# Turning half of a softmax's probabilities on VectorE and by copies inside SBUF, in a decoder layer's cross-attention

## The chip, the core and the metric

The kernel runs on one core of one Trainium2 chip. The metric is the device time of one execution in microseconds (us). Engines are named as the profile names them: PE is TensorE (matrix products and transposes), PEld its weight loads, DVE is VectorE, ACT is ScalarE, POOL is GpSimd, SP is SyncE, which here only issues transfers (DMAs). SBUF is the memory on the chip with 128 partitions, PSUM the memory into which PE writes.

## What is computed

One decoder layer in fp32 on `x` of shape (8, 256, 1024), B = 8 batch elements of S = 256 rows, E = 1024 columns, in three stages. Each adds its result to `x` after a layer norm.

```python
x = x + self_attention(layernorm(x))            # 32 heads, weights by their signs
x = x + cross_attention(layernorm(x), ctx)      # 16 heads, low rank
x = x + ffn(layernorm(x))                       # gate and up, 2752 wide, low rank

# cross_attention(Q, K), for one batch element
C_q, C_kv = Q @ Wq_d, K @ Wkv_d                 # 256 x 128, 256 x 64
CqWqk = (C_q @ W_qk).reshape(n, 16, 64)
scores = einsum('nhl,kl->hnk', CqWqk, C_kv) / sqrt(64)
attn = softmax(scores, axis=-1)                 # 16 heads of 256 x 256
V_up = (C_kv @ Wv_u).reshape(nkv, 16, 64)
out = einsum('hnk,khd->nhd', attn, V_up)
```

The kernel multiplies the probabilities by `C_kv` first and by `Wv_u` after that. The matrix product sums over partitions, so the probabilities, which the softmax leaves with the queries n on the partitions, must first be turned so that the keys k lie there. The change is about how they are turned.

## The kernel before

All rows are handled in tiles of P = 128, TB = 2 of them for each batch element. The order of every engine's work is written out by hand: the program records the instructions under a manual schedule, and each engine runs its own in that order, waiting on semaphores where it needs another's result. A transfer counts on one of eight semaphores of its queue kind, used in turn; it waits until the transfer eight places earlier has landed.

**The loop.** The attention of both kinds goes by `step` (L733), one for four heads: 64 steps of self-attention (b = 0 to 7, c = 0 to 7), then 32 of cross-attention (b = 0 to 7, c = 0 to 3), called from the loop at L1658. A step computes the scores of its own four heads (`cur`), turns the probabilities of the step before (`prev`) and finishes the step before that (`due`). In the order of the code, a step of the cross-attention is:

- PE: the scores of four heads, 16 matmuls into four banks `pss0` to `pss3` that have one buffer each (L676); they wait until the exponentials of the step before have read these banks.
- DVE: `due.early()`, a copy of `po` from PSUM to `ol` (L709); then the row maxima `nm` of the four heads (L743).
- PE: `turned` for the four heads of `prev` (L575): four transposes of 128 x 128 each (L579) into `ps_pt`; ACT copies each to SBUF as `pT` (L583), four buffers.
- PE: `due.late()`: `ol` times Wv_u into `ps_o` (L716); DVE multiplies by one over the sums (`y`, L724), POOL adds to the rows `x1t` (L731). `y` has two buffers.
- ACT: eight exponentials with their sums (L762), `cur.p`, mixed with the parts by a count of PE's time (`sc` and `pe`).
- The parts of the plan, from a queue that `cross_plan` (L1501) fills: for the next batch element the turn of the context and of the normed rows by DVE in blocks of 32 x 32 (`turn32`, L185), `ps_k` and `ckv` (L855, L868), `ps_q` and `cq` (L925, L930), `ckvT` (L877, L880), and `ps_qk` and `cqk` (L941, L944), whose copies go to DVE and ACT in turn. c = 0 has two of the four products `ps_qk` and the turn of the context, c = 1 has `ps_k`, c = 2 has `ps_q`, c = 3 has `ckvT` and the other two `ps_qk`. In b = 0, 1 and 2, output projections of the self-attention (L547) come on top, in b = 7 factors of the feed-forward (L1123).
- DVE: one over the sums (L688).
- PE: `prev.weighted` (L693): `po` = turned probabilities times `ckvT`, 16 matmuls (L699).

**Transfers of the cross-attention.** Before the change SP issues all but the stores of finished rows (`x_leave`, L950, on POOL): the context by quarters (`quarters_load`, L168), the rows `x1t` (L831), the copy of each half of `ckv` to the other half's partitions, SBUF to SBUF (L869), the normed rows to DRAM (L894) and back by quarters (L168), and the feed-forward's weights.

**Feed-forward.** It starts after the last step; its `unit`s take the `pT` buffers for `ac2` (L1220).

Of the kernel before, what the change touches and what calls it, by code (L numbers as in the profile page):

```python
# [18 lines left out]
P = 128  # L19
# [16 lines left out]
def decoder_layer(  # L36
# [67 lines left out]
    dve, act = nc.vector.tensor_copy, nc.scalar.copy  # L104

# [59 lines left out]
    def quarters_load(dst, rows, w=EQ):  # L165

        for k in range(Q4):
            nc.sync.dma_start(  # L168
                dst[32 * k : 32 * k + 32],
                rows[:, k * w : (k + 1) * w].rearrange("(a q) e -> q a e", q=32),  # L170
            )

    def rows_load(dst, rows):

        for k in range(Q4):
            nc.sync.dma_start(
# [74 lines left out]
    def load_x(b):  # L251
        out = []
        for t in range(TB):
            xs = xin.tile([P, E], F32, tag="xin", name="xs")
            nc.sync.dma_start(xs, xf[b * TB + t])
# [9 lines left out]
    def scales_load():  # L265
        for gh in range(2):
            nc.sync.dma_start(
# [3 lines left out]
        nc.sync.dma_start(prow[8:10, :], ks.rearrange("(c p) -> c p", p=P))  # L271
        nc.sync.dma_start(prow[10:12, :], vs.rearrange("(c p) -> c p", p=P))
        nc.sync.dma_start(prow[12:20, :], os_.rearrange("(c p) -> c p", p=P))
# [46 lines left out]
    def weight_load(i):  # L320
        a = blocks[i]
        a.w = wk_.tile([P, E], F32, tag=where[i], name="w")
        if a.q:
            gh, r = a.t // 4, a.t % 4
            for j in range(4):
                r0 = ((gh * 4 + j) * 4 + r) * HD
                nc.sync.dma_start(a.w[j * HD : (j + 1) * HD, :], a.rows[r0 : r0 + HD, :])
        elif a.o:

            rows = a.rows[a.t * P : (a.t + 1) * P, :]  # L330
            for c in range(EC):
                nc.sync.dma_start(
# [3 lines left out]
        else:  # L336
            nc.sync.dma_start(a.w, a.rows[a.t * P : (a.t + 1) * P, :])
# [237 lines left out]
    def turned(p):  # L575
# [6 lines left out]
        pT = wk_.tile([P, TB, S], F32, tag="pT", name="pT", bufs=4)  # L582
        nc.scalar.copy(pT, ps)  # L583
        return pT

    class Self:


        def __init__(self, st, c):
            self.st, self.c = st, c  # L590
# [72 lines left out]
    class Cross:  # L663


        def __init__(self, st, c):
            self.st, self.c = st, c
# [25 lines left out]
        def weighted(self, pTs):  # L693

            self.po = pso.tile([P, 2, S], F32, tag="pso", name="po")
            for i in range(2):
                for k in range(TB):
                    for j in range(2):
# [3 lines left out]
                            pTs[2 * i + j][:, k, :],  # L702
# [4 lines left out]
        def early(self):  # L707
            self.ol = wk_.tile([P, 2, S], F32, tag=("oh0a", "oh0b")[self.c % 2], name="ol")
            nc.vector.tensor_copy(self.ol, self.po)  # L709
# [23 lines left out]
    def step(cur, prev, parts, extra=None):  # L733
# [4 lines left out]
        due = prev.prev if prev is not None else None  # L738
        if due is not None:
            due.early()  # L740
        pTs = []
        for j in range(4):
            nc.vector.tensor_reduce(nm[:, j, :], s[j], AX.X, ALU.max, negate=True)  # L743
            if prev is not None:
                pTs.append(turned(prev.p[j]))
# [13 lines left out]
        def exp(j, t):  # L759
# [5 lines left out]
            )  # L765

# [30 lines left out]
        if prev is not None:  # L797
            prev.weighted(pTs)
# [7 lines left out]
    def cross_weights():  # L806
# [9 lines left out]
        nc.sync.dma_start(xw.wqk, wqk)  # L816
        for i in range(2):
            rows_load(xw.wkvd[:, :, i, :], wkvd)
        for j in range(2):
            nc.sync.dma_start(  # L820
# [4 lines left out]
    def cross_x(st):  # L825
# [3 lines left out]
        for t in range(TB):  # L829
            xs = wt.tile([P, E], F32, tag=f"qw{2 * (st.b % 3) + t}", name="x1t")  # L830
            nc.sync.dma_start(xs, x1[st.b * TB + t])  # L831
# [17 lines left out]
    def ckv_part(st):  # L849
        def main():  # L850
# [14 lines left out]
            for t in range(TB):  # L865
# [3 lines left out]
                nc.sync.dma_start(st.ckv[there, cols], st.ckv[here, cols])  # L869
# [14 lines left out]
    def lnx_parts(st):  # L884

        def send(t):
            need(st)
            g = st.b * TB + t
            for h in range(2):
# [4 lines left out]
                nc.sync.dma_start(n2[g][:, h * 512 : (h + 1) * 512], xn)  # L894
# [22 lines left out]
    def cq_part(st):  # L917
        box = {}

        def main(half):  # L920
# [7 lines left out]
            if half:  # L928
                st.cq = wk_.tile([P, S], F32, tag="v", name="cq", bufs=2)
                nc.vector.tensor_scalar_mul(st.cq, ps, 1.0 / 8.0)  # L930
# [920 lines left out]
```

## Time and profile before

| | us |
|---|---|
| median of 3 runs | 1462.55 |
| lowest and highest | 1459.47, 1462.96 |
| the profiled execution, its own time | 1462.0 |
| its span, first to last instruction | 1460.2 |

| engine | busy us | share of the span |
|---|---|---|
| PE | 1422.7 | 97% |
| DVE | 1073.5 | 74% |
| PEld | 954.7 | 65% |
| ACT | 849.6 | 58% |
| POOL | 610.5 | 42% |

The page gives each engine's busy time, then groups of equal instructions: line, engine, operation, output<-input, shapes, count, then busy time and mean duration of one, then idle time ahead of them and what ended it. The timeline lists an engine's instructions in order of time: start, duration, engine, line, operation, count, and in brackets the idle time before and what released it. Matmuls overlap one another, so the duration of one is longer than the time from one to the next. The mean granted clock of PE is 0.993 of full speed. The scores of the cross-attention start between 629.1 and 948.7 us, and its last `po` ends at 974.

### The profile page before, as it was taken

How to read it: one execution, taken by the hardware profiler on the slowest of the kernel's cores; microseconds unless marked ns; L12 is line 12 of the kernel's file. 1: busy time of each engine (PE TensorE's matmuls, PEld its weight loads, DVE VectorE, ACT ScalarE, POOL GpSimd, SP SyncE). 2: the span in 40 equal slices, each digit the busy share in tenths (PEclk: the TensorE clock that was granted, in tenths of full speed). 3: DMA queues.
4: the chain of work that ended last, by engine and by line, in shares of the span. 5: the costliest groups of instructions: out<-in, count | busy, mean ns of one | idle time of the engine just before them, and what ended most of it. 6: DMA issues, size and time to landing. Idle time of an engine off the chain costs nothing.

```text
span 1460.2 us, 25787 instructions
## 1 busy us (share of the span) xinstructions
PE 1422.7 (97%) x8946; PEld 954.7 (65%) x8946; DVE 1073.5 (74%) x2042; ACT 849.6 (58%) x2553; POOL 610.5 (42%) x769
## 2 busy tenths in 40 slices
PE   6899999999999999989999999999999999999998
PEld 6778888888888888667787777654444444444444
DVE  6888898989898989866777778447747645555664
ACT  4777898989898988856556666543313322223320
POOL 2544444444444443402232262435525424555740
PEclk9999999999999999989999999999999999999999
DMA  9620010101010124344448676723222000213003
GB/s 213 135 59 16 30 59 30 59 30 59 31 62 27 45 63 163 105 103 130 134 128 271 199 249 175 230 89 131 84 61 72 29 0 34 82 58 129 1 0 116
DMA packets 102961, 134.75 MB, mean 92 GB/s; under 512 B 44538, under 2 KB 75440, under 8 KB 102704
## 3 DMA queue, kind: packets, MB, share of 16 engines
q1 hardware_dynamic: 98224, 116.33, 27.2%
q0 software_dynamic: 4608, 16.78, 3.0%
q8 instruction: 72, 1.18, 0.3%
q14 instruction: 57, 0.47, 0.1%
HBM read 90.60 MB, written 41.94 MB: 91 GB/s over the span
## 4 chain that ended last, share of the span: by engine, by line
PE 54%; ACT 2%; DVE 2%; DMA 1%; issue 1%; SPq 0%; POOL 0%; ACTq 0%; DVEq 0%
PE c L1189 17%; PE z L1283 9%; PE ps_pt L579 4%; PE ps_o L1399 4%; PE s L676 4%; PE ps_p L1123 4%; PE po L699 3%; PE ps_o L716 2%; PE ps_q L925 2%; PE ps_qk L941 2%; ACT p L762 2%; PE ps_k L855 1%; PE ps_o L547 1%; PE ps_h L1252 0%; DMA n<-xn 0%
## 5 line engine op out<-in xcount | busy, mean ns | idle before, releaser
L762 ACT ACTIVATE p<-s,nm 128x256 f32<-128x256 f32 x768 | 358.4, 518 | 3.3 <-DVE nm L743 3.3
L583 ACT COPY pT<-ps_pt 128x512 f32<-128x512 f32 x384 | 197.7, 600 | 146.1 <-PE ps_pt L579 146.1
L743 DVE TENSOR_REDUCE nm<-s 128x2 f32<-128x512 f32 x384 | 237.5, 679 | 5.0 <-PE s L676 3.7
L579 PE MATMUL ps_pt<-ident,p 128*128 128x128 f32 x1536 | 198.9, 282 | 5.8 <-DVE p L623 2.5
L579 PEld LDWEIGHTS ps_pt<-ident,p 128*128 128x128 f32 x1536 | 167.4, 143 | 46.2 <-issue 24.2
L762 ACT ACTIVATION_READ_ACCUMULATOR p<-s,nm 128x1 f32 x768 | 191.8, 250 | 0.0
L1240 POOL TENSOR_TENSOR ac<-ac,sg 128x512 f32<-128x512 f32 x41 | 52.2, 1273 | 207.5 <-ACT sg L1239 207.5
L731 POOL TENSOR_TENSOR x1t<-x1t,y 128x256 f32<-128x256 f32 x64 | 46.3, 743 | 200.5 <-DVE y L724 200.5
L407 POOL TENSOR_SCALAR tmp<-y 128x512 f32<-128x512 f32 x78 | 60.1, 770 | 167.4 <-DVE y L556 91.3
L1189 PE MATMUL c<-t,s_v 128*128 128x512 f32 x252 | 122.2, 594 | 1.1 <-ACT q L1213 0.8
L454 PE MATMUL ps_q<-xh,qT_w 128*128 128x256 f32 x496 | 122.4, 288 | 0.0
L454 PE MATMUL ps_q<-xl,qT_w 128*128 128x256 f32 x496 | 119.6, 282 | 0.0
L1199 ACT COPY a<-c 128x512 f32<-128x512 f32 x42 | 24.6, 585 | 153.6 <-PE c L1189 153.6
L547 PE MATMUL ps_o<-oT_w,oh 128*128 128x512 f32 x256 | 106.4, 416 | 0.0
L547 PE MATMUL ps_o<-oT_w,ol 128*128 128x512 f32 x256 | 101.7, 397 | 0.0
L454 PEld LDWEIGHTS ps_q<-xh,qT_w 128*128 128x128 f32 x496 | 93.5, 188 | 1.6
L454 PEld LDWEIGHTS ps_q<-xl,qT_w 128*128 128x128 f32 x496 | 93.7, 189 | 0.0
L623 DVE TENSOR_SCALAR p<-p,sm 128x256 f32<-128x256 f32 x256 | 86.7, 396 | 8.4 <-PE ps_q L454 0.5
L1189 PEld LDWEIGHTS c<-t,s_v 128*128 128x128 f32 x252 | 47.4, 190 | 62.6 <-issue 50.3
L630 ACT ACTIVATE p<-p,sm 128x256 f32<-128x256 f32 x172 | 75.8, 513 | 18.9 <-DVE sm L613 18.3
L1221 DVE SCALAR_TENSOR_TENSOR ac<-c,b_col,q 128x512 f32<-128x512 f32 x42 | 31.5, 751 | 65.9 <-ACT q L1219 65.9
L600 PE MATMUL s<-kT,qT 32*128 32x256 f32 x1024 | 76.4, 403 | 3.7 <-DVE qT L412 2.4
(194 smaller groups left out, 3081.5 us busy)
## 6 DMA issues: line engine op xcount, KB each, us to landing
xs<-in_x_dram SPq DMA_DIRECT2D x32, 512.0 KB
x<-xs POOLq DMA_DIRECT2D x16, 512.0 KB, 3.1
x1t<-x SPq DMA_DIRECT2D x16, 512.0 KB
c<-in_ctx_dram SPq DMA_DIRECT2D x64, 128.0 KB
n<-xn SPq DMA_DIRECT2D x32, 256.0 KB
xp<-n SPq DMA_DIRECT2D x64, 128.0 KB
x<-x1t POOLq DMA_DIRECT2D x16, 512.0 KB, 5.6
x2n<-x SPq DMA_DIRECT2D x16, 512.0 KB
```

Source lines behind the costliest of these rows:

```text
L407: nc.gpsimd.tensor_scalar(tmp, y, 0.0, -1e6, ALU.min, ALU.max)
L454: nc.tensor.matmul(ps[:, i, :], w(i, e), x_[:, e, :], start=(e == 0 and x_ is st.xh), stop=(e == EC - 1 and x_ is st.xl),)
L547: nc.tensor.matmul(ps, o_[c // 4][:, c % 4, t * P : (t + 1) * P], oT_w[:, c, h * 512 : (h + 1) * 512], start=(c == 0 and o_ is st.oh), sto ...
L579: nc.tensor.transpose(ps[:, k, t * P : (t + 1) * P], p[:, t, k * P : (k + 1) * P], ident)
L583: nc.scalar.copy(pT, ps)
L600: nc.tensor.matmul(s[j][:, t, :], st.qT[p0 : p0 + 32, c, t * P : (t + 1) * P], st.kT[p0 : p0 + 32, c // 4, :], start=True, stop=True,)
L623: nc.vector.tensor_scalar_mul(p, p, self.sm[:, t, j : j + 1])
L630: nc.scalar.activation(p, p, AF.Copy, scale=self.sm[:, t, j : j + 1])
L743: nc.vector.tensor_reduce(nm[:, j, :], s[j], AX.X, ALU.max, negate=True)
L762: nc.scalar.activation(cur.p[j][:, t, :], s[j][:, t, :], AF.Exp, bias=nm[:, j, t : t + 1], accum_out=cur.sm[:, t, j : j + 1],)
L1189: nc.tensor.matmul(ps, w, x_, start=start, stop=stop, skip_group_check=True)
L1283: nc.tensor.matmul(db.X[key], w, x_, start=start, stop=stop or key == "1")
```

## The change

In the cross-attention, heads 0 and 1 of each step are no longer turned by PE. As soon as their exponentials are given out, `turned_blocks` has DVE transpose them in blocks of 32 x 32 into a tile `pB` (tag `oh0b`, one buffer). Sixteen copies on SP's queue, each of 32 partitions with 1 KB, then bring the blocks from partitions 32a of `pB` to partitions 32c of `pD`, which alternates between the tag `oh0a` and one of the two buffers of `pT`. Heads 2 and 3 are turned by PE as before; `pT` is now a pair in one tile of two buffers. `weighted` reads `pD` with a stride (`keys_of`), takes heads 2 and 3 first, and in the cross-attention is moved from the end of the step to the next step, behind its scores. `ol` is copied by ACT, as are `cq` and all of `cqk`. All other transfers of the cross-attention that SP had issued are issued by POOL (`way`). In the feed-forward, `ac2` is taken from pairs, the last one from the tag `cq`.

```diff
+    way = [nc.sync]
...
         for k in range(Q4):
-            nc.sync.dma_start(
+            way[0].dma_start(
...
-    def turned(p):
+    both = [None]
+
+    def turned(p, j):
...
-        pT = wk_.tile([P, TB, S], F32, tag="pT", name="pT", bufs=4)
+        if j % 2 == 0:
+            both[0] = wk_.tile([P, 2, TB, S], F32, tag="pT", name="pT", bufs=2)
+        pT = both[0][:, j % 2]
         nc.scalar.copy(pT, ps)
         return pT
 
+    crossed = [0]
+
+    def turned_blocks(cur):
+
+        n = crossed[0]
+        crossed[0] += 1
+        pB = wk_.tile([P, 4, 2, 4, 32], F32, tag="oh0b", name="pB")
+        for j in range(2):
+            src = cur.p[j].rearrange("p t (k c e) -> p c (t k) e", k=TB, c=4)
+            nc.vector.transpose(pB[:, :, j], src)
+        shape = [P, 4, 2, TB, TB, 32]
+        if n % 2:
+            pD = wk_.tile(shape, F32, tag="oh0a", name="pD")
+        else:
+            pD = wk_.tile(shape, F32, tag="pT", name="pD", bufs=2)
+        for d in range(4):
+            for a in range(4):
+                c = (a + d) % 4
+                nc.sync.dma_start(
+                    pD[32 * c : 32 * c + 32, a].rearrange("p j t k q -> p (j t k q)"),
+                    pB[32 * a : 32 * a + 32, c].rearrange("p j m q -> p (j m q)"),
+                )
+        for j in range(2):
+            cur.blocks[j] = pD[:, :, j]
+
+    def keys_of(pT, k):
+        if len(pT.shape) == 3:
+            return pT[:, k, :]
+        return pT[:, :, :, k, :].rearrange("p a t q -> p t a q")
+
+    def turned_of(prev, j):
+        return prev.blocks[j] if j in prev.blocks else turned(prev.p[j], j)
...
             self.po = pso.tile([P, 2, S], F32, tag="pso", name="po")
-            for i in range(2):
+            for i in (1, 0):
...
-                            pTs[2 * i + j][:, k, :],
+                            keys_of(pTs[2 * i + j], k),
...
         def early(self):
-            self.ol = wk_.tile([P, 2, S], F32, tag=("oh0a", "oh0b")[self.c % 2], name="ol")
-            nc.vector.tensor_copy(self.ol, self.po)
+            self.ol = wk_.tile([P, 2, S], F32, tag="v", name="ol", bufs=2)
+            nc.scalar.copy(self.ol, self.po)
...
+        if isinstance(due, Cross):
+            due.weighted(due.pTs)
         if due is not None:
             due.early()
...
-                pTs.append(turned(prev.p[j]))
+                pTs.append(turned_of(prev, j))
...
+            if (j, t) == (1, TB - 1) and not divided:
+                turned_blocks(cur)
...
         if prev is not None:
-            prev.weighted(pTs)
+            if isinstance(prev, Self):
+                prev.weighted(pTs)
+            prev.pTs = pTs
...
-                st.cq = wk_.tile([P, S], F32, tag="v", name="cq", bufs=2)
-                nc.vector.tensor_scalar_mul(st.cq, ps, 1.0 / 8.0)
+                st.cq = wk_.tile([P, W], F32, tag="cq", name="cq")[:, 0:S]
+                nc.scalar.activation(st.cq, ps, AF.Copy, scale=1.0 / 8.0)
...
-        ac2 = wide("pT", "ac2", 4)
+        if k == FULL - 1:
+            ac2 = wide("cq", "ac2", 1)
+        else:
+            if k % 2 == 0:
+                both[0] = wk_.tile([P, 2, W], F32, tag="pT", name="ac2", bufs=2)
+            ac2 = both[0][:, k % 2]
...
-        k, q, t, u = ckv_part(x_), cq_part(x_), ckvT_part(x_), cqk_parts(x_, (dve, act))
+        k, q, t, u = ckv_part(x_), cq_part(x_), ckvT_part(x_), cqk_parts(x_, (act, act))
...
+            way[0] = nc.gpsimd if kind is Cross else nc.sync
```

## The prediction

> **What bounds the kernel now.** Three stages follow one another: self-attention to 629 us, cross-attention (32 steps, four to a batch element b, c = 0 to 3) from 629 to about 972 us, the feed-forward to the end. The change acts in the second. I read the page first: PE is busy for 97% of the span and the chain that ended last runs over PE, so a cross step ends when PE is through it. Then the timeline of PE for two steps, then that of ACT, DVE and SP over the same stretch.
>
> ```profile
> PE 1422.7 (97%) x8946; PEld 954.7 (65%) x8946; DVE 1073.5 (74%) x2042; ACT 849.6 (58%) x2553; POOL 610.5 (42%) x769
> ...
> L579 PE MATMUL ps_pt<-ident,p 128*128 128x128 f32 x1536 | 198.9, 282 | 5.8 <-DVE p L623 2.5
> ```
>
> ```profile
> 797.69 2.28 PE L676 MATMUL s<-ckv,cqk 64*128 64x256 f32 x16
> 799.91 2.04 PE L579 MATMUL ps_pt<-ident,p 128*128 128x128 f32 x16
> 801.79 1.15 PE L716 MATMUL ps_o<-w_up,ol 128*128 128x128 f32 x8
> 802.78 1.89 PE L941 MATMUL ps_qk<-cq,w_up 128*128 128x256 f32 x8
> 804.60 1.95 PE L699 MATMUL po<-pT,ckv 128*64 128x256 f32 x16
> 806.48 2.74 PE L676 MATMUL s<-ckv,cqk 64*128 64x256 f32 x16
> ```
>
> A step is scores (L676) 1.9 to 2.0, the 16 transposes (L579) 1.9, ps_o 1.1, the part of the next element 1.9 to 3.6, po 1.9, with hardly a hole; the scores stretch to 2.28 and 2.74 where they wait for ACT (7.8 us in 19 waits in all).
>
> ```profile
> 804.71 0.58 ACT L944 COPY cqk<-ps_qk 128x512 f32<-128x512 f32 x1 [1.09 <-PE ps_qk L941]
> ...
> 809.90 2.05 ACT L583 COPY pT<-ps_pt 128x512 f32<-128x512 f32 x4 [1.86 <-PE ps_pt L579]
> 811.81 0.51 ACT L762 ACTIVATE p<-s,nm 128x256 f32<-128x256 f32 x1
> 812.18 0.23 ACT L762 ACTIVATION_READ_ACCUMULATOR p<-s,nm 128x1 f32 x1
> 812.27 0.50 ACT L762 ACTIVATE p<-s,nm 128x256 f32<-128x256 f32 x1
> ```
>
> ```profile
> 814.89 2.48 DVE L185 STREAM_TRANSPOSE xT<-xp 128x512 f32<-128x512 f32 x4
> ```
>
> Four pT copies take 2.05 (0.5 each); exponentials start every 0.45, eight take 3.6. A DVE transpose of 128x512 takes 0.62. From the starts of the scores I take the step lengths. From 668.68 (b=0, c=3) to 910.22 there are 25 steps; two (c=2 at 695.69 and 736.64, with an output projection) last 13.94, the other 23 sum to 241.5 - 27.9 = 213.7 us, mean 9.29. Around them: 15.9 and 9.6 (b=0, c=0 and 1), 14.1 (c=2), and in b=7 15.65, 13.64, 6.77, 14.58.
>
> **The change on PE.** Per step, 8 of 16 transposes go: 0.95 us. Step 0 turns the last self heads and keeps 16. Taken alone: 31 x 0.95 = 29.5 us off. ACT loses two pT copies (1.0) and gets the ol copy and one more cqk copy every second step (0.58 each); DVE loses ol (0.64) and gets two transposes of p (1.3). None of the three engines is full by that.
>
> **What it puts in its place: a loop through SP.** pB has one buffer (tag oh0b, bufs=1). The transposes into pB in a step stand behind exp (1,1), and their DVE instruction waits for all eight DMA semaphores, that is until the 16 copies of the step before have read pB. The copies themselves wait for those transposes. So two steps can't lie closer than: two transposes 1.3 + hand-over 0.1 + 16 issues on SP + landing of the last + wake-up. Behind the waiting transpose stand, on DVE, the reciprocal and the four row maxima of the next step, so the next exponentials and scores wait too.
>
> The trace has no such copy of 32 rows. The nearest is the copy of half of ckv, SBUF to SBUF with two-dimensional sides and 32 KB, like the new ones; next, quarter loads from DRAM, 128 KB:
>
> ```profile
> L869 SPq DMA_DIRECT2D ckv<-ckv x16: 467/530/570, 626.6 to 890.1; - x16
> ```
>
> ```profile
> L168 SPq DMA_DIRECT2D c<-in_ctx_dram x64: 311/430/767, 564.8 to 851.8; - x64
> ```
>
> ```profile
> 643.58 1.11 SPq L869 DMA_DIRECT2D ckv<-ckv  x2
> 644.74 3.91 SPq L168 DMA_DIRECT2D c<-in_ctx_dram  x8
> ```
>
> The columns after the count are min/median/max ns. Two ckv copies take 1.11 (0.555 each with the gap), eight quarter loads 3.64 to 3.91 (0.46 to 0.49). Bounds for one issue: 0.35 (the shortest quarter load, 0.302 to 0.311, and a gap of 0.05) to 0.59 (the second of a ckv pair, 0.542, and the gap). I take 0.53, at the ckv row, as it is the only SBUF-to-SBUF one, slightly lower for half the rows: 16 x 0.53 = 8.5. Landing: of the pair issued until 644.69, the last packets in the trace end at 645.7: 1.0 us. Below nothing is excluded, a copy can't land before it is issued; the upper end is what the stretch at 790 shows behind eight loads (issue over at 791.39, PE released at 793.69): 2.3. Eight semaphores on one DVE instruction: 0.3, an estimate from PE's 51 ns per extra semaphore wait (0 to 0.5). Sum: 1.3 + 0.1 + 8.5 + 1.0 + 0.3 = **11.2 us a step**; bounds 1.3 + 0.1 + 5.6 + 1.0 + 0 = 8.0 and 1.3 + 0.1 + 9.4 + 1.3 + 0.5 = 12.6.
>
> The Trainium skill, "DMA: Bandwidth & Descriptors", Rules for kernel authors, speaks against such pieces: "Coalesce into one large transfer; under 64 KB you're paying mostly overhead". Its section on the anatomy of one DMA gives about 2.0 us fixed for a GpSimd transfer, where this trace has 1.0 from the end of issue to the landing on SP's; by 2.0 the step would be 12.2 and the total some 25 us higher.
>
> **Sum.** The 23 short steps: 23 x 11.2 - 213.7 = +43.9. b=0 c=1: 9.6 to 11.2, +1.6. b=7 c=2: 6.77 to 11.2, +4.4. The six long steps are over 11.2 and keep PE as their bound: -0.95 each, -5.7. Together +44.2. The profiled execution took 1462.0 us (span 1460.2); the median of the runs is 1462.55, the same within 0.04%. 1462 + 44 = **1506 us**.
>
> **The other edits, hidden in this sum.** po moves from the end of a step to behind the next scores, ol to ACT: this lengthens ACT's own loop, see the first rival. The strided reading of pD by po: no row shows it; between nothing and twice the 0.94 of two heads, and not below nothing, as no work goes. 8.35 us of PE in 11.2 cover even the twofold. POOL gets some 24 issues per element; its own 512 KB stores cost 0.55 to 0.64 there, so 24 x 0.6 = 14.4 beside 5.6 of adds and 2 of the rest, in 45 us. In order behind a waiting issue stand the adds of y (two buffers, so a lag of a step and a half) and rs; the tightest reader is the turn of xT two steps (22 us) after the sends, whose 4 issues, landing (median 5.6), 8 issues and landing make 18. Without this cover: 2 to 5 us an element, most likely in b=5 and 6, where POOL also norms (3.8 each). SP loses all these. The feed-forward writes its ac2 into pairs of the same four slots, whose readers end in the same unit as before: nothing, up to 0.3 us for each of 20 pairs if not. cq on ACT: 0.45 in c=2, in the rival's loop.
>
> **Clock.** After 2.55 us without work at 632 us, the trace grants 0.5 from 634.73 to 644.97, and eight transposes take 2.41 instead of 1.0:
>
> ```profile
> 634.77 2.41 PE L579 MATMUL ps_pt<-ident,p 128*128 128x128 f32 x8 [2.55 <-DVE p L623]
> ```
>
> PE will idle 11.2 - 8.35 = 2.85 a step. One stretch of 3.41 us (the shortest at 0.5 in this trace) at half clock adds 1.7: 10.05, still under 11.2, nothing. Two add 3.4: 11.75, +12 us in 23 steps. I take nothing for the sum and 12 for the range. The Trainium skill, "TensorE: Matmul & The Clock Gate", The HAM clock gate, says the throttled state is the default and a busy window of about 3.4 us releases it; the row agrees, and by that rule a gap in each step could throttle each step.
>
> **Rivals.**
>
> *ACT's loop decides* (issues at 0.40 or less). From the end E of a step's exponentials: second half of the scores 1.0, po 1.9, hand-over 0.1, ol 0.58, two pT 1.0, exponentials 3.6: 8.2 (c=1). In c=0 both cqk copies stand ahead of six exponentials and the first needs PE up to 1.0 + 1.9 + 1.0 + 1.1 + 0.95: 5.95; with 0.1, copy, two exponentials, copy and six more, 10.75. In c=3 the same with ps_kt (0.3) and five at the end: 10.6. In c=2, 8.55 on PE, cq 0.45, hand-over, two exponentials: 10.0. Short steps: 6 x 10.75 + 6 x 8.2 + 4 x 10.0 + 7 x 10.6 = 228, +14.2; the rest -0.9 + 1.4 - 5.7: +9, 1471 us. For it: ACT already ends the waits of the scores. Against: ckv's 0.53.
>
> *PE's gain comes through* (the other side: faster). A loop under 8.35 us needs issues at 0.35, the shortest load's, on SP that then issues nothing else; and ACT's order must not hold the scores, so that copies of cqk cost less than worked out. Then 1462 - 29.5 = 1432.
>
> *Slower still*: the upper bounds together, 12.1 to 12.6 a step, with the half clock or the GpSimd queue late: 23 x 12.1 - 213.7 = +65, +2.5, +5.3, -5.7: 1529; with 12 to 15 of clock and POOL, 1544.
>
> That the change doesn't do what it says is excluded for the counts: 512 copies stand in the SP order, 16 a step.
>
> **How the numbers follow.** Loop through SP, 1485 to 1525: 0.62. Slower still: 0.13. ACT's loop, 1462 to 1484: 0.15, a third of it within 0.3% (4.4 us, about what a measurement tells from no change). PE's gain: 0.10. So slower 0.85 (0.62, 0.13 and 0.10 of the ACT loop), same 0.05, faster 0.10. The range leaves out the gain and the far end: 1466 to 1546.
>
> **What would show it.** Right: on DVE, a wait ahead of the first transpose into pB in nearly each short step, ended by the copies' landing; SP busy with 16 issues of 0.5 back to back, 8 to 9 us, and then at once again a step later; starts of scores 11 apart in short steps of any c; PE at three quarters there. Wrong: issues of 0.35 or less; the wait ahead of pB ended by ACT; the scores waiting for ACT in c=0 and 3 alone (ACT's loop); xT or y on DVE waiting for POOL's transfers (the queue).

## The result and the profile after

The changed kernel takes 1633.5 us (median of 4 runs, 1631.9 to 1636.2), the kernel before 1462.6: a ratio of 1.118, 95% interval 1.117 to 1.120. The forecast was 1506, with 1546 as its upper end. The sign was right, and the 171 us are almost four times the forecast's 44.

Self-attention ends at 629 us in both traces, and the feed-forward takes 488.2 us before and 488.0 after. The whole loss lies in the cross-attention, 343 us before and 513 after. The page of the changed kernel, three parts of it: busy times, the clock in 40 slices, and the chain that ended last by engine and by line.

```profile
PE 1467.1 (90%) x8690; PEld 966.9 (59%) x8690; DVE 1082.5 (66%) x2052; ACT 850.4 (52%) x2543; POOL 730.0 (45%) x985
...
PEclk9999999999999998888878788798999999999999
...
PE 34%; SPq 15%; DMA 9%; DVE 3%; issue 2%; ACT 1%; POOL 0%; DVEq 0%; ACTq 0%; POOLq 0%
PE c L1233 15%; SPq L609 14%; DMA pD<-pB 8%; PE z L1332 8%; PE ps_o L1448 3%; PE ps_p L1167 2%; PE po L737 2%; PE ps_pt L582 1%; DVE pB L600 1%; PE s L714 1%; ACT p L802 0%; PE ps_h L1301 0%; DMA n<-xn 0%; DVE nm L783 0%; PE ps_k L899 0%
```

PE has 256 instructions fewer and is busy 44 us longer, while its granted clock falls to 0.7 and 0.8 in the second third (0.83 on the average of the cross-attention, 0.99 before). The chain now runs over SP's issues of the copies (L609, 14% of the span) and their landing (8%): together more than the whole loss. The groups of the page name the two who wait for it, and whom these hold up in turn:

```profile
L600 DVE STREAM_TRANSPOSE pB<-p 128x512 f32<-128x512 f32 x64 | 41.7, 690 | 211.8 <-DMA pD<-pB 196.1
...
L747 ACT COPY ol<-po 128x512 f32<-128x512 f32 x32 | 18.8, 587 | 231.3 <-PE po L737 231.3
...
L737 PE MATMUL po<-pD,ckv 128*64 128x256 f32 x256 | 49.0, 517 | 98.6 <-DMA pD<-pB 98.6
```

DVE stands 196 us ahead of the transposes into `pB`, PE 99 us ahead of the `po` of heads 0 and 1, and ACT 231 us ahead of `ol`, which needs that `po`. The issues on SP, from the view of their line (the columns are min/median/max ns):

```profile
L609 SPq DMA_DIRECT2D pD<-pB x512: 507/589/1539, 646.6 to 1139.6; - x171
...
DMA to landing us min/median/max: 1.7/2.2/13.0
```

Two steps in the timeline of DVE, and PE's over the same stretch (start, duration, instruction, and in brackets the idle time before and its releaser):

```profile
810.91 1.30 DVE L600 STREAM_TRANSPOSE pB<-p 128x512 f32<-128x512 f32 x2 [6.05 <-DMA pD<-pB]
...
834.51 1.30 DVE L600 STREAM_TRANSPOSE pB<-p 128x512 f32<-128x512 f32 x2 [14.42 <-DMA pD<-pB]
...
849.16 1.31 DVE L600 STREAM_TRANSPOSE pB<-p 128x512 f32<-128x512 f32 x2 [2.49 <-DMA pD<-pB]
```

```profile
810.97 1.98 PE L737 MATMUL po<-pD,ckv 128*64 128x256 f32 x8 [4.36 <-DMA pD<-pB]
...
823.11 1.08 PE L737 MATMUL po<-pT,ckv 128*64 128x256 f32 x8
834.53 1.98 PE L737 MATMUL po<-pD,ckv 128*64 128x256 f32 x8 [10.34 <-DMA pD<-pB]
...
843.85 1.08 PE L737 MATMUL po<-pT,ckv 128*64 128x256 f32 x8
849.19 1.08 PE L737 MATMUL po<-pD,ckv 128*64 128x256 f32 x8 [4.25 <-DMA pD<-pB]
```

DVE's transposes and PE's `po` come free within 0.06 us of each other: the same landing holds both. PE has done the first half of `po` (from `pT`, 1.08 us) by 844.93 and then stands 4.25 us. At 810.97 and 834.53, after 4.4 and 10.3 us without work, the next eight matmuls take 1.98 in place of 1.08, at a granted clock of 0.50; at 849.19, after 4.25, they take 1.08, and the clock falls only after that (0.50 from 850.2 to 853.5 us).

**The loop, taken apart.** For each of the 31 periods between the transposes of one step and of the next I took four times from the trace, and beside them the end of exponential (1,1), which the transposes also need. Shortest and mean are each row's own:

| part of a period, us | forecast | shortest | mean |
|---|---|---|---|
| two transposes and the hand-over to SP | 1.4 | 1.31 | 1.37 |
| from the first issue to the end of the last | 8.5 | 10.00 | 10.84 |
| from there to the next transposes | 1.3 | 1.56 | 3.37 |
| period | 11.2 | 12.93 | 15.58 |

The exponential was done 1.7 to 14.3 us before the transposes began, in all 31. The profile names the copies as what ended DVE's wait in 29 of them (the 196 us above) and an ACT copy in two steps of b = 7. By the landing times in the trace the transposes begin 0.32 us after the last of the sixteen copies has landed in all 31, those two included. The chain that ended last has one such landing and what follows it (start, duration):

```profile
845.91 2.93 DMA pD<-pB
...
849.16 1.32 DVE pB L600 x2
```

So the copies held every step, the long ones too: 31 x 15.58 = 483 of the stage's 513 us.

### The profile page after: what moved, and what is told of

Read it like the earlier page. It is cut to its first block, busy times and chain, and to the rows that moved or that the text cites. A ratio compares the mean times of both kernels' runs of the same rounds, so it can differ in the third digit from the quotient of the medians.

```text
span 1630.0 us, 25931 instructions
## 1 busy us (share of the span) xinstructions
PE 1467.1 (90%) x8690; PEld 966.9 (59%) x8690; DVE 1082.5 (66%) x2052; ACT 850.4 (52%) x2543; POOL 730.0 (45%) x985
## 4 chain that ended last, share of the span: by engine, by line
PE 34%; SPq 15%; DMA 9%; DVE 3%; issue 2%; ACT 1%; POOL 0%; DVEq 0%; ACTq 0%; POOLq 0%
PE c L1233 15%; SPq L609 14%; DMA pD<-pB 8%; PE z L1332 8%; PE ps_o L1448 3%; PE ps_p L1167 2%; PE po L737 2%; PE ps_pt L582 1%; DVE pB L600 1%; PE s L714 1%; ACT p L802 0%; PE ps_h L1301 0%; DMA n<-xn 0%; DVE nm L783 0%; PE ps_k L899 0%
## 5 line engine op out<-in xcount | busy, mean ns | idle before, releaser
L588 ACT COPY pT<-ps_pt 128x512 f32<-128x512 f32 x320 | 168.1, 596 | 60.2 <-PE ps_pt L582 59.6
L582 PE MATMUL ps_pt<-ident,p 128*128 128x128 f32 x1280 | 184.2, 299 | 5.7 <-DVE p L661 2.5
L802 ACT ACTIVATION_READ_ACCUMULATOR p<-s,nm 128x1 f32 x768 | 188.1, 245 | 0.0
L582 PEld LDWEIGHTS ps_pt<-ident,p 128*128 128x128 f32 x1280 | 152.8, 152 | 51.2 <-issue 29.8
L600 DVE STREAM_TRANSPOSE pB<-p 128x512 f32<-128x512 f32 x64 | 41.7, 690 | 211.8 <-DMA pD<-pB 196.1
L747 ACT COPY ol<-po 128x512 f32<-128x512 f32 x32 | 18.8, 587 | 231.3 <-PE po L737 231.3
L737 PE MATMUL po<-pD,ckv 128*64 128x256 f32 x256 | 49.0, 517 | 98.6 <-DMA pD<-pB 98.6
L714 PE MATMUL s<-ckv,cqk 64*128 64x256 f32 x512 | 94.9, 435 | 14.7 <-ACT p L802 14.5
L737 PEld LDWEIGHTS po<-pD,ckv 128*64 128x64 f32 x256 | 22.8, 177 | 119.0 <-issue 116.7
```

Of the source, the lines that this page charges most:

```text
L582: nc.tensor.transpose(ps[:, k, t * P : (t + 1) * P], p[:, t, k * P : (k + 1) * P], ident)
L714: nc.tensor.matmul(s[2 * i + j][:, t, :], st.cqk[p0 : p0 + XD, 2 * c + i, t * P : (t + 1) * P], st.ckv[p0 : p0 + XD, :], start=True, stop= ...
L737: nc.tensor.matmul(self.po[XD * j : XD * (j + 1), i, :], self.st.ckvT[:, k, :], keys_of(pTs[2 * i + j], k), start=(k == 0), stop=(k == TB ...
L802: nc.scalar.activation(cur.p[j][:, t, :], s[j][:, t, :], AF.Exp, bias=nm[:, j, t : t + 1], accum_out=cur.sm[:, t, j : j + 1],)
```

## The experiments

My theory: the loop through SP sets the step, its size is issues times their pitch plus the landing, and the landing and some issues are stretched by other transfers. The rivals: the place of `po` behind the scores costs the time whatever the copies do; GpSimd's queue is the cost; the copies are slow by their bytes, not by their number. The table gives each kernel's median and its ratio to the kernel before, run on the same chip.

| kernel | us | ratio, 95% |
|---|---|---|
| only the queue moved | 1468.3 | 1.003 to 1.007 |
| only ACT's copies added | 1470.2 | 1.005 to 1.008 |
| only `po` moved | 1497.1 | 1.023 to 1.026 |
| these three together, PE turns all heads | 1523.4 | 1.040 to 1.046 |
| changed, eight copies | 1512.7 | 1.034 to 1.038 |
| the same, `po` at the end of its step | 1527.5 | 1.042 to 1.047 |
| changed, blocks in every second step | 1570.7 | 1.072 to 1.078 |
| changed, copies on two queues | 1583.3 | 1.082 to 1.085 |
| changed, two `pB` | 1588.5 | 1.084 to 1.090 |
| changed, few other transfers in b = 3 to 5 | 1599.1 | 1.093 to 1.097 |
| changed, a quarter of the other transfers left out | 1616.2 | 1.104 to 1.108 |
| through DRAM, all on SP | 1586.5 | 1.084 to 1.087 |
| through DRAM, the others on GpSimd | 1560.6 | 1.067 to 1.070 |

### The parts of the change without the copies

**PE turns all heads.** The changed kernel without its blocks and copies:

```diff
-            if (j, t) == (1, TB - 1) and not divided:
-                turned_blocks(cur)
```

> The changed kernel without the two transposes into pB and the 16 copies: PE turns all four heads again; po behind the next scores, ol, cq and cqk on ACT and the GpSimd queue stay. Theory (the loop pB, 16 copies, landing, pB carries the loss: 15.6 us a step in the trace of the changed kernel): the loss of 171 us goes but for ACT's longer order, 1465 to 1505. Rival 1 (ACT's order with po behind the scores is the larger part): 1540 or more, with the scores waiting for ACT in every step. Rival 2 (the GpSimd queue is late and holds DVE): 1520 or more, with waits of xT or xn for transfers.

It took 1523.4: the blocks and copies cost 110 of the 171 us, and 62.6 stand without them. That is well above what I expected of the rest, and in the range of the second rival, the queue; so I took the rest apart. (This kernel also keeps the pairs of `pT` and the order of the heads in `po`.)

**The queue alone**, in the kernel before:

```diff
+            way[0] = nc.gpsimd if kind is Cross else nc.sync
```

> The kernel before with one part of the change alone: all transfers of the cross-attention on GpSimd's queue. Theory: hidden, 1460 to 1470. Rival (the queue is late, in order behind the adds of y): 1480 or more, with DVE waiting for xT, cT or xn ahead of its parts.

1468.3, +7.5. By the starts of the scores, 5.2 of it lie in one step, b = 3, c = 3, which lasts 14.60 in place of 9.45, and 0.8 each in c = 3 of b = 4 and 5. In the long one DVE's norm waits for adds on POOL, which stand in its order behind eight loads of the context:

```profile
790.48 0.69 DVE L141 BATCH_NORM_STATS2 st<-x1t 128x6 f32<-128x512 f32 x1 [5.10 <-POOL x1t L732]
```

The granted clock is 0.5 there from 793.8 to 800.6 us, which adds to it. So GpSimd's order does hold up other engines, but in a few steps only.

**The place of `po` alone**, and **ACT's copies alone**, each in the kernel before:

```diff
+        if isinstance(due, Cross):
+            due.weighted(due.pTs)
         if due is not None:
             due.early()
```

> The kernel before with one edit: po of a step goes behind the scores of the next step. No copies, no change of queue, ol, cq and cqk as before. Theory (the order is the cost: scores, po, ol, and only then the transposes; half of ACT's pT copies and all exponentials then start about 2 us later in the step): 1485 to 1515 us, that is most of the 55 us by which the kernel with PE turning all heads stood over the one with only the queue moved; waits of the scores for ACT's exponentials grow from 7.8 us to over 40. Rival (ACT's added copies are the cost): 1460 to 1475.

```diff
-            nc.vector.tensor_copy(self.ol, self.po)
+            nc.scalar.copy(self.ol, self.po)
...
-                nc.vector.tensor_scalar_mul(st.cq, ps, 1.0 / 8.0)
+                nc.scalar.activation(st.cq, ps, AF.Copy, scale=1.0 / 8.0)
...
-cqk_parts(x_, (dve, act))
+cqk_parts(x_, (act, act))
```

> The kernel before with one edit: ol, cq and all of cqk copied by ACT; po stays at the end of its step, queue as before. Theory (the order behind the scores is the cost, not the copies): 1462 to 1478 us; ol is taken at the start of a step, when ACT has little to do, and the cqk copies push six exponentials back by 0.6 us in c = 0 and c = 3. Rival (ACT's copies are the cost): 1485 to 1520, with the scores waiting for ACT in c = 0 and 3.

1497.1 (+36.1) and 1470.2 (+9.1): the place of `po` is the cost, ACT's copies are a small one. The waits of the kernel with only `po` moved, on PE and its loads, from 645 to 990 us (engine, line, for whom: us in total, times, longest):

```profile
PEld s L676 <- ACT p L764: 29.9, 55, 1.4
```

```profile
PE s L676 <- ACT p L764: 12.2, 27, 1.0
```

The loads of the scores' weights wait 29.9 us for the exponentials, 7.8 before; the waits of PE's matmuls (12.2) lie inside these and don't add to them. That is 22 of the 36 us, and less than the 40 that I had expected. Two stretches at a granted clock of 0.50 (778.6 to 785.3 and 908.3 to 915.0 us; before, none after 645 us) take some more: c = 1 lasts 5.1 and 5.2 longer than before in b = 3 and 6, where they lie, and 1.7 to 2.0 longer in b = 1, 2, 4 and 5. The rest I did not place. With `po` between the scores and the transposes, ACT gets its `pT` copies and with them the exponentials about 2 us later in each step, and the next scores need the exponentials. The three edits alone sum to 36.1 + 9.1 + 7.5 = 52.7; together they cost 62.6. The last 10 I did not take apart (the pairs of `pT` and the order of heads are in them too); the mean clock from 629 to 990 us is 0.92 with the three together and 0.97 with only `po` moved.

### The loop

**Eight copies.** The same bytes in half as many issues:

```diff
-        for d in range(4):
-            for a in range(4):
-                c = (a + d) % 4
+        for c in range(4):
+            for h in range(2):
+                g = (c + h) % 2
                 nc.sync.dma_start(
-                    pD[32 * c : 32 * c + 32, a].rearrange("p j t k q -> p (j t k q)"),
-                    pB[32 * a : 32 * a + 32, c].rearrange("p j m q -> p (j m q)"),
+                    pD[64 * g : 64 * g + 64, c].rearrange("p j t k q -> p (j t k q)"),
+                    pB[64 * h : 64 * h + 64, c].rearrange("p j m q -> p (j m q)"),
                 )
```

> The changed kernel with 8 copies of 64 partitions (64 KB each) a step in place of 16 of 32 partitions: the same bytes, half the issues. The blocks are laid at other places than the mathematics needs, so its output is not the layer's. Theory (SP's time for each issue is on the loop, and it doesn't grow with the size): issues of 0.6 to 0.7, loop 1.3 + 8 x 0.65 + 3.4 = 10, under what the order of PE and ACT asks (10.6 to 14.7 in the kernel with PE turning all heads): 1480 to 1530 us. Rival (the time follows the bytes, the queue can't take more): 8 issues of 1.1 to 1.3 and 1600 to 1640.

1512.7: 121 of the 171 us go with eight issues of sixteen. The view of the issues' line, and DVE's timeline over one period:

```profile
L609 SPq DMA_DIRECT2D pD<-pB x256: 461/595/1742, 644.6 to 1011.7; - x128
```

```profile
849.57 1.31 DVE L600 STREAM_TRANSPOSE pB<-p 128x512 f32<-128x512 f32 x2 [0.86 <-ACT p L802]
...
858.35 1.30 DVE L600 STREAM_TRANSPOSE pB<-p 128x512 f32<-128x512 f32 x2 [0.41 <-DMA pD<-pB]
```

The median issue is 595 ns for 64 KB, 589 for 32 KB: the pitch belongs to the issue, not to the bytes. The period shown is 8.78 long, of which the eight issues take 5.61; at the shortest they take 4.93, and the shortest period is 7.98. Such a loop no longer decides every step: the first of these transposes waits for ACT, and the 31 periods last 11.67 on the average. What is left over the kernel before (51.7) is 11 less than what the three edits cost without any copy (62.6). By this difference of two kernels about a third of the 29.5 us of transposes taken from PE shows with eight issues; what late copies and the clock still cost in it is not separated.

**`po` back at the end of its step.** From the kernel with eight copies, with `ol`, `cq` and `cqk` as before:

```diff
-        if isinstance(due, Cross):
-            due.weighted(due.pTs)
...
-            if isinstance(prev, Self):
-                prev.weighted(pTs)
-            prev.pTs = pTs
+            prev.weighted(pTs)
```

> The kernel with eight copies of 64 partitions (blocks at other places than the mathematics needs, so its output is not the layer's), and besides po back at the end of its step, ol, cq and cqk copied as before; the other transfers stay on GpSimd's queue. Theory (of the 50 us by which the kernel with eight copies stands over the kernel before, po's place and ACT's copies are most; without them PE's saving shows, less 7.5 us of the queue): the copies are down 1.3 + 5 + 1.7 = 8 us after the exponentials of heads 0 and 1, some 5 us into the next step, po comes at 7.4; 1440 to 1470 us. Rival (any way over transfers is too late for the same step's po when other loads lie beside it, as in the versions through DRAM): 1490 to 1560 us, with PE waiting at po for the landing.

1527.5, slower than with `po` late, and the rival's number. In quiet steps the gain is there: c = 3 of b = 0 to 2 lasts 7.91, against 8.96 before. In 15 steps PE waits at `po` for the landing, as its waits show:

```profile
PE po L737 <- DMA pD<-pB: 62.7, 15, 7.8
```

So the late place buys something, but no place of `po` tried here pays for a transfer between two steps.

**Two `pB`**, in turn from b = 3 on (the second takes a place which weights of the feed-forward give up until the stage's end):

```diff
-        pB = wk_.tile([P, 4, 2, 4, 32], F32, tag="oh0b", name="pB")
+        pB = wk_.tile([P, 4, 2, 4, 32], F32, tag="oh1b" if n >= 12 and n % 2 else "oh0b", name="pB")
```

> The changed kernel with a second buffer for pB from element 3 on (20 of 32 steps; one weight tile of the feed-forward is loaded later to make room). Theory (the wait of the transposes for the copies of the step before sets the step): in these 20 steps the wait of DVE ahead of pB falls from about 6.5 us a step to under 2, the next bound is SP's issuing, 16 x 0.633 = 10.1 a step, so 20 x (15.6 - 10.7) = 98 us less where no bulk load lies between, about 1535 to 1560. Rival (landings behind the traffic of the GpSimd queue set the step, however many buffers): 1600 or more, with po waiting for pD as before.

1588.5, between theory and rival. The waits, from 645 to 1070 us:

```profile
DVE pB L600 <- DMA pD<-pB: 83.4, 15, 13.9
PE po L737 <- DMA pD<-pB: 63.4, 18, 9.9
```

DVE's wait for the copies falls to 83 us in 15 waits, from 196 in 29, but SP still issues 10 us or more a step, and PE waits at `po` for the landing of the same copies. One buffer was a part of the loop and not all of it; the issues and the landing stay.

**Blocks in every second step:**

```diff
+        if n % 2 == 0:
+            return
         pB = wk_.tile([P, 4, 2, 4, 32], F32, tag="oh0b", name="pB")
```

> The changed kernel with blocks and copies in every second step only (PE turns all four heads of the others). Theory: the loop of 13 to 16 us lies in two steps of 9 to 10 us and is hidden; left are 16 x 0.95 us of PE won and ACT's longer order, so some 10 to 15 below the run in which PE turns all four, 1455 to 1495. Rival (not the loop, but the copies' load on the DMA engines and the half clock cost the time): half of the loss stays, 1530 or more.

1570.7, a clear miss: the rival's number. SP issues only in every second step now, and still the kernel is 47 us over the one without blocks. The trace shows why: in b = 4 and 5 steps are 9.9 to 10.6 and 14.8 to 20.1 long in turn. In one of the long ones SP's last issue ends at 856.6, and PE's timeline has

```profile
864.42 1.97 PE L739 MATMUL po<-pD,ckv 128*64 128x256 f32 x8 [4.58 <-DMA pD<-pB]
```

7.8 us later. From 840 to 870 us the transfers were these (queues: packets, MB, share of the 16 engines; issues: count, size, median us to landing):

```profile
q0 software_dynamic: 1600, 5.08, 60.2%
...
pD<-pB SPq DMA_DIRECT2D x16, 32.0 KB, 4.7
```

So one batch of copies, 1.4 + 10 + up to 8 us, is by itself too long for the `po` that reads it, when GpSimd's transfers fill the engines. The half clock, which the rival names too, is not separated by this run. My expectation had counted the engine's free time and forgotten the latency of one batch.

**Copies on two queues**, eight by SP and eight by GpSimd:

```diff
-                nc.sync.dma_start(
+                (nc.sync if d < 2 else nc.gpsimd).dma_start(
```

> The changed kernel, with eight of the sixteen copies of a step issued by GpSimd and eight by SP; bytes, order and results as in the changed kernel. Theory (issue time on one queue is the largest part): 8 x 0.63 = 5 us of issue on each, loop 1.3 + 5 + 3.5 = 10, or a little more where GpSimd is also busy with the other transfers: 1510 to 1550 us, close to the kernel with eight copies (1513). Rival (the copies are slow at landing, whatever queue issues them): 1590 to 1640.

1583.3, between theory and rival and nearer the rival. SP's part does take 5.4 us on the average, but GpSimd's stands in its order behind the other transfers, each of which may wait for another. Its timeline:

```profile
862.49 0.50 POOL L609 DMA_DIRECT2D pD<-pB  x1 [1.01 <-DMA v1b<-in_L_ffn_V_dram]
863.74 0.50 POOL L609 DMA_DIRECT2D pD<-pB  x1 [0.75 <-DMA v1b<-in_L_ffn_V_dram]
```

These copies wait until a weight load has landed that stands eight places earlier on the same queue, and so has the same semaphore. The mean from SP's last issue to the next transposes is 7.2 us.

### What stretches issue and landing

**A quarter of the other transfers left out**:

```diff
+        if st.b >= 3:
+            st.c = xts[2].c
+            return
...
+                if st.b < 3:
+                    way[0].dma_start(n2[g][:, h * 512 : (h + 1) * 512], xn)
...
+            if st.b >= 3:
+                st.xp = xts[2].xp
+                return
```

> The changed kernel, but elements b = 3 to 7 of the cross-attention don't load their context, don't send their normed rows and don't load them back; they take those of b = 2, so the output of these elements is not the layer's. About 20 of 24 GpSimd issues an element go. Theory (the copies land 3 to 4.4 us after the last issue, instead of 1.6, because other transfers lie beside them): the loop falls by about 2 us in the steps from b = 1 on, 1585 to 1605 us. Rival (landing depends on the copies' own queue, or po's place sets the step anyway): within 10 us of the changed kernel, 1623 to 1640.

1616.2: 17 us less than the changed kernel, between theory and rival. GpSimd's queue still moved 40.3 MB from 645 to 1100 us, 53.4 in the changed kernel, and the landing fell only from 3.37 to 3.10. That did not settle it, so one more kernel left two elements nearly without other transfers.

**Few other transfers.** Besides the edits above:

```diff
+            st.x = xts[st.b - 3].x
+            return
...
-                ffn_load_a()
                 ffn_bias_load()
-            if b == 4:
-                ffn_load_b(0)
+            if b == 6:
+                ffn_load_a()
+        if (b, c) == (6, 1):
+            ffn_load_b(0)
```

> The changed kernel with hardly any other transfer in elements b = 3 and 4 and few in b = 5: elements from 3 on don't load their context, their rows or their normed rows and don't send these (they take those of earlier elements, so their output is not the layer's), and the feed-forward's weights are loaded in b = 6 instead of b = 3 and 4. What stays are the stores of finished rows (512 KB, two in c = 1 of each element) and the copies of ckv. Read from the trace: in the changed kernel the transposes into pB start 3.4 us after the last issue on the average, 1.56 at the shortest, in all 31 steps held by the copies. Theory (the 1.8 us over the shortest, and the issues over 10.0, come from other transfers beside the copies): 1.6 to 2.0 us and 10.0 to 10.3 in most steps of b = 3 and 4, more only by the stores; steps there 12.9 to 13.5 apart. Rival (they come from something else, from the queue itself or from DVE): a mean of 3 us in these steps as before.

DVE's timeline in b = 3, c = 2 and 3, and b = 4, c = 0:

```profile
840.32 1.30 DVE L600 STREAM_TRANSPOSE pB<-p 128x512 f32<-128x512 f32 x2 [3.66 <-DMA pD<-pB]
...
853.31 1.30 DVE L600 STREAM_TRANSPOSE pB<-p 128x512 f32<-128x512 f32 x2 [5.78 <-DMA pD<-pB]
...
866.29 1.30 DVE L600 STREAM_TRANSPOSE pB<-p 128x512 f32<-128x512 f32 x2 [6.25 <-DMA pD<-pB]
```

12.99 and 12.98 apart: 1.37 + 10.0 + 1.61. From 812 to 893 us the time from the last issue to the next transposes is 1.55 to 1.61 in each of six periods; the issues take 10.0, and 11.8 and 10.7 only in the two periods beside the stores of finished rows. In the period after these six it is 4.4, beside four loads of 512 KB. Theory, then. The opposite end is the changed kernel's period from 810.91 to 834.51, whose transfers were, from 811 to 835 us:

```profile
q0 software_dynamic: 1323, 5.84, 81.0%
...
w_ffn<-in_L_ffn_V_dram POOLq DMA_DIRECT2D x1, 2752.0 KB, 14.2
...
pD<-pB SPq DMA_DIRECT2D x16, 32.0 KB, 8.9
```

Here GpSimd's queue, a load of 2.75 MB among its transfers, takes 81% of the engines' time; the sixteen issues take 18.1 us, and a copy lands 8.9 us after its issue (median), against 1.9 from 815 to 905 us in the kernel with few other transfers. So the landing of a copy goes by what else the 16 engines carry. The Trainium skill, "DMA: Bandwidth & Descriptors", Queues, rings and completion order, gives a reason that would fit: a transfer's semaphore is raised only after every earlier write of the same DMA engine, whatever its queue. These runs show the delay; none separates that reason from plain waiting for a turn.

### A version without the loop

**Through DRAM.** Heads 0 and 1 are stored by one transfer each and come back by four quarter loads, six issues in all; DVE turns them on arrival, `po` at the end of its step:

```diff
+        nc.sync.dma_start(
+            cur.way[:, :, j, :], cur.p[j].rearrange("p t s -> p (t s)").rearrange("p (c f) -> p c f", c=4)
+        )
+        if j == 1:
...
+            for c in range(4):
+                nc.sync.dma_start(
+                    cur.pq[32 * c : 32 * c + 32],
+                    cur.way[:, c].rearrange("(a q) j f -> q a j f", q=32),
+                )
```

> A version meant to keep what the change wants from PE without its loop. Heads 0 and 1 of a cross step go to DRAM as soon as their exponentials are written (ACT writes them in the order that the way back needs), 256 KB each, and come back by four quarter loads of 128 KB: 6 issues a step in place of 16, all on SP's queue with the other transfers, two buffers for what comes back. DVE turns the blocks on arrival, and po stays at the end of its step, as before; ol on ACT, cq and cqk as before. Theory (what cost the time was the number of issues on the loop, po's place and the GpSimd queue; none is here): SP 6 x 0.6 + the old 24 x 0.5 an element = 6.6 us a step beside PE's 8.4; PE gets 0.95 us less in 31 steps, so 1435 to 1455 us. Rival (the way through DRAM lands too late for po at the end of the step, 3 + 4.5 us and SP's order, so PE waits): 1475 to 1530.

The second version has, besides:

```diff
+            way[0] = nc.gpsimd if kind is Cross else nc.sync
```

> The same as the version through DRAM, with the other transfers of the cross-attention on GpSimd's queue, as the change has them; SP has only the probabilities. Theory: SP's order holds up the other loads by its waits (each load back waits for the store to land), so this one differs from the version with all on SP by the GpSimd queue's +7.5 us less what that order costs: 1440 to 1465 us. Rival (SP's order costs more than that): faster than the version with all on SP.

1586.5 and 1560.6, both slower than the kernel before: the first goes the rival's way and beyond its range (1530), the second is the rival's. In the first one, PE's waits and SP's from 645 to 1000 us:

```profile
PE po L739 <- DVE pD L617: 93.8, 25, 11.2
```

```profile
SPq L609 <- DMA pw<-p: 103.9, 30, 7.3
```

SP waits for each store to land before it can issue the loads back, and PE waits for the blocks in 25 steps. On GpSimd's queue the others no longer stand behind that wait, which saves 26 us, more than the 7.5 of that queue. In that version PE's wait is

```profile
PE po L739 <- DVE pD L617: 77.3, 25, 8.4
```

With few issues the number is no longer the trouble: two landings of 4.9 and 4.3 us (medians in the second version) in a row come before the blocks. No version that beats the kernel before came out of these runs.

## Why the prediction was right in sign and wrong in size

- **"Loop through SP", 11.2 us a step.** The mechanism is shown: the transposes begin 0.32 us after the last copy's landing in all 31 periods, sixteen issues take SP 10 us or more, and eight issues fewer take 121 us off. The step that failed is the size of two of its terms. **The issues, "16 x 0.53 = 8.5"**: 10.0 at the least, 10.84 on the average. I had put the pitch below the `ckv` row "for half the rows", but the number of rows does not matter (595 and 589 ns at twice and once the size); the upper bound, 0.59, lay below the 0.63 that sixteen in a row show, and the `ckv` row's own longest, 570 ns, would have given 0.62 with the gap. **The landing, 1.0, and the wake-up, 0.3**: the wake-up was right (0.32); the landing took 1.24 at the least and 3.06 on the average. I had the row for the higher end, 2.3 behind eight loads, though GpSimd issues such loads in most steps; and in the sum of the upper bounds I then put 1.3 in its place, so that the 12.6 should have been 13.6. Both terms were mis-sized in the same way, by rows from quiet stretches and short bursts. Of the 4.4 us a step that the loop lasted longer than forecast, 1.7 are in its shortest period already (1.5 of them in the issues), and 2.65 come above it: 0.84 in the issues and 1.81 in the landing. In the kernel with few other transfers both are all but gone in the quiet stretch from 812 to 893 us, but for the stores: they come from the transfers beside the copies.
- **The six long steps "keep PE as their bound", -5.7.** Wrong. Less their 0.95 they were 12.7 to 14.7 long, above 11.2 but not above the 15.6 that the loop takes.
- **The sum.** For the 25 steps that the forecast gave to the loop, 25 x (15.58 - 11.2) = 110 us are missing in it; for the six others, forecast at 13.35 on the average, 6 x 2.2 = 13. Together 123, and 127 were missing.
- **ACT's loop, with `po` and `ol`, "hidden in this sum".** In the changed kernel it is: all 31 periods are set by the copies. But alone the place of `po` costs 36 us. The first rival had that chain right (scores, `po`, `ol`, transposes, exponentials) and its price wrong: the kernel with eight copies has a loop as short as that rival asked for, and takes 1513, not 1471. The rival left out the queue's 7.5 and the copies that still land late (in that kernel PE waits 20 us for them and DVE 54, from 645 to 960 us), and counted a full clock. How the 42 us between divide among these is not shown.
- **The strided reading of `pD` by `po`**, forecast at nothing to 0.94 more a step. Nothing: 1.08 us for eight matmuls from `pD` and from `pT` alike (843.85 and 849.19; the clock is at 1.00 until 850.2).
- **GpSimd's queue, counted as hidden.** Alone +7.5, most of it in one step. In the sum its real price was another: its transfers stretch the copies.
- **`ac2` in pairs, counted as nothing.** Right: the feed-forward takes 488.2 and 488.0 us.
- **The clock, "I take nothing for the sum".** The clock falls after waits, as in the row at 632 us, to a mean of 0.83 in the cross-attention (0.99 before), but the copies hold the step, and their loop (transposes on DVE, issues, landing) has no instruction of PE, so it is not what sets the time here. How much it adds where the loop is short, as in the three edits without copies, stays open.
- **The other side, PE's gain** (1432): its condition, issues of 0.35 or less, did not come. With eight copies the loop is 7.98 us at the shortest and 11.67 on the average, and a third of the gain showed.

## What to carry to other kernels

When a step's data must go out by transfers and come back within the next step, add up one batch from end to end (issues times their pitch, landing beside the busiest neighbours, wake-up) and hold it against the step; free time on the issuing engine or few bytes do not help. Price the landing from the stretch of the trace where the transfer engines are fullest, not from the quietest row. And check what an edit that "makes room" for the latency costs by itself: here the place of `po` alone lost more than the transposes could ever give.

## What the runs showed of the hardware

- Sixteen copies from SBUF to SBUF, issued back to back by SP, take 10.0 us, 0.63 each, with 32 KB; eight with 64 KB take 4.94, 0.62 each. The Trainium skill, "DMA: Bandwidth & Descriptors", Issuing engines are not separate DMA queues, calls the sequencer's time to start a transfer usually small relative to the transfer itself. One copy here takes 0.59 us to issue and 1.7 at the least from the start of its issue to its landing; but the landings overlap and the issues don't, so a batch is 10.0 us of issue and 1.56 from the last issue to the waking of DVE.
- Issue is not independent of the transfers either: 18.1 us for sixteen beside the 2.75 MB load in the changed kernel, 11.8 beside two stores of 512 KB in the kernel with few other transfers.
